# Layer 0's norms of pairs 2 to 4 applied to rows as they lie, in a bidirectional recurrence with a ternary feed-forward block

## The chip, the core and the metric

The kernel runs on one core of a Trainium2 chip. The core has five engines that work through their own instruction streams in order and wait for each other by semaphores: PE (TensorE, matrix products and transposes), DVE (VectorE), ACT (ScalarE), POOL (GpSimd) and SP (SyncE, which here only issues DMAs). The metric is the device time of one execution in microseconds. Before the change it was 1712.66 us, the median of 3 runs (1712.62 to 1712.66).

## The reference, cut to what matters

The input x is 8 sequences of 512 tokens with 512 channels. Three things are added up:

```python
x = x + xcond(layernorm(x))        # two stacks of 4 gated recurrent layers, one forward, one backward in time
x = x + ffn(layernorm(x))          # 512 -> 2048 -> 512, weights rounded to -1, 0, 1

def mingru(h, Wz, bz, Wh, bh):     # Wz = Wh and bz = bh here
    z = sigmoid(h @ Wz.T + bz);  a = clip(1 - z, 1e-8, 1 - 1e-8)
    return scan(a, z * tanh(h @ Wh.T + bh))      # s_t = a_t s_(t-1) + b_t along the tokens

def stack(h):
    for i in range(4):
        new = mingru(h, ...)
        if i > 0: new = new + h
        h = layernorm(new) * gamma + beta        # over the 512 channels of each token
    return h
```

All arithmetic is in float32. Both directions of a stack use the same weights, so in layer 0 they also share their products.

## The kernel before, in words

**Layout.** The recurrence keeps a sequence with channels on the 128 partitions and tokens along the row: 4 chunks of 128 channels by 512 tokens, since the scan of DVE runs along a row. A layernorm needs sums over channels, which lie across partitions. So a norm turns the 4 chunks round: for each of 4 tiles of 128 tokens, `turned` (L316) makes 4 transposes on PE into a PSUM tile `pt`, `stats` (L171 to L182) finds mean and variance on DVE and the power -1/2 on POOL, `normalise` (L188, L189) writes the token tile `tok` on ACT, and `back` (L325, L331) turns the 4 tiles into 4 channel chunks `pf` on PE and applies gamma and beta on ACT while it writes them to the state. A turn of one tile and a back of one chunk are 4 transposes of 128x128 each.

**Slots.** The order of the work is written out by the program, in slots (`slot`, `shares`, `queue`). A slot first emits its own work, mostly one chunk of a layer (`gates`, L487: 4 float32 products, recorded as 8 MATMULs, then two sigmoids and a tanh on ACT and the clip on POOL), then what is due in the list `stages`, then its shares: from the queue `turns` and from the queue `backs` each one piece if it is ready, and a second one if that is late (its time plus its piece number has come; `cap` is 2 in a slot of the fusion). After the shares come, on DVE, the product z*t (L514), the scan (L518) and the residual addition (L588) of the chunk. What DVE gets in a slot's shares is thus ahead of that slot's scan. A token tile that `last` writes in one slot can be turned back from the next slot on.

**Pairs.** The 8 sequences go in 4 pairs, and each pair has 4 streams (b, 0) and (b, 1), (b+1, 0) and (b+1, 1): sequence and direction. A layer takes 4 slots for each stream, so 16 for a pair. Between two pairs lies a transition: `fusion` of the old pair (8 tiles, L622, 16 MATMULs each, with two scaled additions L632 on DVE) is interleaved with `first_layer` of the new one (8 chunks, L535, with a scaling L546 and two scans). Numbered from the transition's start, slots 0 to 15 hold, in order, F C C F C F C C F C F C F C F F (F a tile of the fusion, C a chunk of layer 0). Slots 16 to 19 are layer 1 of the new pair's stream (b, 0), slots 20 to 23 of (b, 1), and so on. Layer 0's four norms run in slots 8 to 23: before the change (b, 0) and (b, 1) are turned in slots 8 to 12 and turned back in 11 to 15; (b+1, 0) and (b+1, 1) are turned in slots 15 to 19 and turned back in 18 to 23. Layer 1 of (b, 0) is next: its norm is queued for slot 21, is turned in slots 21 to 24, and its first chunk is turned back in slot 25.

**Buffers that tie the engines together.** `pt` has 2 PSUM tiles, `u` (the products) 4, the gate's tile `t` 2 and `a` 3, the tiles z 16, the token tiles `tok` 10.

**Other work in the order.** The rows of a sequence's own layernorm before layer 0 reduce to one factor for each token, `scale` (`scale_x`): 4 transposes of a broadcast column and one copy on ACT. For pairs 3 and 4 its statistics (`norm_x`) are found on DVE during layer 1 and 2 of the pair before, one tile in 4 slots from slot 21 on. The last norm of a stream (`norm_last`) needs only 1/sigma for each token; `by_scalar` finds it on ACT in two passes (L396 to L398), `tokens` on DVE. Rounding the feed-forward weights is cut into 68 steps (`extra`, done by `pieces(n)`): 32 sums, 4 for the two thresholds, 32 roundings. A rounding is two DVE instructions (L193, L194), with a load ahead and a store behind on SP's queue.

## Time and profile before

| what | value |
|---|---|
| median of 3 runs | 1712.66 us |
| profiled execution | 1712.95 us, its span 1711.2 us, clock granted to PE 1.00 |
| PE busy | 1700.3 us of the span (99%) |
| DVE busy | 1389.1 us (81%) |
| ACT busy | 1089.5 us (64%) |
| POOL busy | 377.2 us (22%) |
| transitions between pairs, slots 0 to 15 | about 262 to 357, 562 to 654, 860 to 952 us |
| feed-forward block | from 1218 us on |

The profile lists groups of instructions as line, engine, operation, `out<-in` by the program's tile names, shapes, count, busy time, mean duration in ns, and the idle time of the engine before them with what ended it. PE's instructions overlap in a pipeline: a MATMUL of 593 ns starts 430 ns after the one before, a transpose of 273 ns 109 ns after the one before, so a time on PE is best taken between starts. A row of the windows view gives a stretch, its length, and each engine's busy time with its count of instructions; a row of the timeline gives start, length, engine, line, operation, tiles and count.

### The profile page before, as it was taken

The numbers are of one execution on the slowest core, as the hardware profiler recorded it, in microseconds if no ns is written. First come the engines' busy times: TensorE is split into PE (matmuls) and PEld (weight loads), VectorE is DVE, ScalarE is ACT, GpSimd is POOL, SyncE is SP. The second block draws the span as 40 slices with busy tenths as digits, with TensorE's granted clock in tenths as the row PEclk, the third lists the DMA queues.
The fourth block names the chain that finished last, engine by engine and source line by source line (L and its number), as shares of the span: only waits on it lengthen the run. The fifth ranks groups of instructions, "written<-read, shape, count | busy, mean of one in ns | idle before, by whom it ended". The sixth has DMA issues, their size and how long they took to land.

```text
span 1711.2 us, 19776 instructions
## 1 busy us (share of the span) xinstructions
PE 1700.3 (99%) x6440; PEld 1042.6 (61%) x6440; DVE 1389.1 (81%) x2619; ACT 1089.5 (64%) x1918; POOL 377.2 (22%) x558
## 2 busy tenths in 40 slices
PE   9999999999999999999999999999999999999999
PEld 5455554555555455555545555554688888888887
DVE  7988889889887888888788888885568768768877
ACT  5898873468886346888535688862356566666654
POOL 3333333223332222333222222321000000000000
PEclk9999999999999999999999999999999999999999
DMA  7002231150000125000012200102201101100100
GB/s 271 19 25 81 98 93 37 66 193 19 13 1 1 56 68 191 19 13 1 1 56 75 98 28 22 75 1 99 74 1 50 50 1 50 50 21 30 50 19 31
DMA packets 46599, 91.75 MB, mean 54 GB/s; under 512 B 5280, under 2 KB 5536, under 8 KB 45472
## 3 DMA queue, kind: packets, MB, share of 16 engines
q1 hardware_dynamic: 45488, 88.78, 15.1%
q10 hardware_dynamic: 1008, 1.70, 0.3%
q8 instruction: 51, 0.84, 0.2%
q14 instruction: 52, 0.43, 0.1%
HBM read 65.30 MB, written 25.17 MB: 53 GB/s over the span
## 4 chain that ended last, share of the span: by engine, by line
PE 92%; DVE 5%; ACT 2%; POOL 1%; issue 0%; DVEq 0%
PE u L487 33%; PE po L937 14%; PE ph L910 14%; PE pu L622 13%; PE u L535 6%; PE pt L316 6%; PE pf L325 4%; DVE z L518 1%; PE py L214 1%; DVE z L514 1%; DVE st L171 1%; ACT tok L189 1%; DVE z L588 1%; PE pst L948 0%; POOL rs L178 0%
## 5 line engine op out<-in xcount | busy, mean ns | idle before, releaser
L487 PE MATMUL u<-xT,gw 128*128 128x512 f32 x768 | 345.5, 593 | 0.0
L487 PE MATMUL u<-h,gw 128*128 128x512 f32 x768 | 345.5, 592 | 0.0
L518 DVE TENSOR_TENSOR_SCAN z<-a,z 128x512 f32<-128x512 f32 x224 | 277.1, 1237 | 21.8 <-DVE z L514 0.9
L511 POOL TENSOR_SCALAR a<-a 128x512 f32<-128x512 f32 x224 | 150.3, 671 | 559.2 <-ACT a L505 558.3
L487 PEld LDWEIGHTS u<-xT,gw 128*128 128x128 f32 x768 | 138.6, 190 | 138.7 <-issue 137.0
L487 PEld LDWEIGHTS u<-h,gw 128*128 128x128 f32 x768 | 138.6, 190 | 138.2 <-issue 138.2
L505 ACT ACTIVATE a<-u,ngb 128x512 f32<-128x512 f32 x192 | 131.7, 686 | 142.4 <-PE u L487 140.9
L937 PE MATMUL po<-pwq,ghi 128*128 128x512 f32 x512 | 202.8, 396 | 0.0
L171 DVE BATCH_NORM_STATS2 st<-pt 128x6 f32<-128x512 f32 x244 | 169.3, 694 | 39.2 <-PE pt L316 32.5
L937 PE MATMUL po<-pwq,glo 128*128 128x512 f32 x512 | 199.7, 390 | 0.0
L910 PE MATMUL ph<-yhi,fcq 128*128 128x512 f32 x512 | 199.7, 390 | 0.0
L910 PE MATMUL ph<-ylo,fcq 128*128 128x512 f32 x512 | 199.4, 389 | 0.0
L514 DVE TENSOR_TENSOR z<-z,t 128x512 f32<-128x512 f32 x224 | 154.8, 691 | 52.6 <-ACT z L507 52.3
L914 ACT ACTIVATE g<-ph 128x512 f32<-128x512 f32 x128 | 76.4, 597 | 186.6 <-PE ph L910 186.6
L178 POOL TENSOR_TENSOR rs<-ve,mhalf 128x1 f32<-128x1 f32 x192 | 125.5, 654 | 155.1 <-DVE nmu L182 152.7
L189 ACT ACTIVATE tok<-pt,nmr,rs 128x512 f32<-128x512 f32 x192 | 149.4, 778 | 6.4
L925 DVE TENSOR_TENSOR acc<-acc,g 128x512 f32<-128x512 f32 x112 | 77.4, 691 | 85.0 <-ACT g L914 84.1
L507 ACT ACTIVATE z<-u,gb 128x512 f32<-128x512 f32 x192 | 132.4, 690 | 0.0
L506 ACT ACTIVATE t<-u,gb 128x512 f32<-128x512 f32 x192 | 130.8, 681 | 0.0
L316 PEld LDWEIGHTS pt<-ident,z 128*128 128x128 f32 x640 | 78.7, 141 | 77.2 <-issue 48.9
L535 PE MATMUL u<-xT,gw 128*128 128x512 f32 x256 | 114.8, 593 | 0.8 <-DVE gw L767 0.8
L622 PE MATMUL pu<-fw,xT 128*128 128x512 f32 x256 | 115.2, 593 | 0.0
(164 smaller groups left out, 2621.0 us busy)
## 6 DMA issues: line engine op xcount, KB each, us to landing
xf<-in_x_dram SPq DMA_DIRECT2D x32, 256.0 KB, 5.5
x<-xf SPq DMA_DIRECT2D x32, 256.0 KB, 2.0
xy<-x SPq DMA_DIRECT2D x32, 256.0 KB, 4.0
xn<-in_x_dram SPq DMA_DIRECT2D x31, 256.0 KB, 4.5
out_dram<-xy SPq DMA_DIRECT2D x31, 256.0 KB, 2.0
xT<-in_xt_dram SPq DMA_DIRECT2D x7, 1024.0 KB, 7.7
fca<-in_fc_wT_dram SPq DMA_DIRECT2D x16, 256.0 KB, 2.9
pwa<-in_proj_wT_dram SPq DMA_DIRECT2D x16, 256.0 KB, 2.6
```

The lines of the kernel that those rows point to most:

```text
L171: nc.vector.bn_stats(st, src)
L189: nc.scalar.activation(dst, src, AF.Identity, bias=nmr, scale=rs)
L316: nc.tensor.transpose(pt[:, ts(c, P)], zs[c][:, ts(t, P)], ident)
L487: nc.tensor.matmul(u, lhsT=gw[l][:, c, ts(o, P)], rhs=h[:, c, :], start=(c == 0), stop=(c == NC_ - 1),)
L507: nc.scalar.activation(z, u, AF.Sigmoid, bias=gb[:, l, o : o + 1])
L511: engine.tensor_scalar(a, a, CLAMP_HI, CLAMP_LO, ALU.min, ALU.max)
L514: nc.vector.tensor_tensor(z, z, t, ALU.mult)
L518: nc.vector.tensor_tensor_scan(dst[:, d], a[:, d], z[:, d], 0.0, ALU.mult, ALU.add)
L535: nc.tensor.matmul(u, lhsT=gw[0][:, c, ts(o, P)], rhs=xT[b][:, c, :], start=(c == 0), stop=(c == NC_ - 1),)
L622: nc.tensor.matmul(pu, lhsT=hs[d][:, c, ts(t, P)], rhs=fw[:, d * NC_ + c, :], start=(c == 0), stop=(c == NC_ - 1),)
L910: nc.tensor.matmul(ph, lhsT=w, rhs=ys[b][c][i], start=(c == 0 and i == 0), stop=(c == NC_ - 1 and i == 1),)
L937: nc.tensor.matmul(po[b][t], lhsT=part[:, ts(t, P)], rhs=pwq[k // NP_][:, k % NP_, :], start=(k == 0 and i == 0), stop=(k == NF - 1 and i ...
```

## The change

For layer 0's norms of sequences 2 to 7, except that of stream (b, 0) where b is even (so three norms in each of pairs 2, 3 and 4, nine in all), `norm_rows` takes the place of `norm`. The turns stay: each tile is still turned into `pt`. Tiles 0 and 1 get their mean and variance on ACT (two passes over the tile), tiles 2 and 3 on DVE, all into one small tile `pk` of 128 x 2 x 4. `close` makes 1/sigma of all four tiles at once (one addition on DVE, one power on POOL). One slot later `send` turns `pk` with a single transpose into 8 short rows, copies them on ACT, writes them to DRAM and reads them back twice as rows of 512 tokens broadcast to all 128 partitions (`to_rows`, three DMAs on SP's queue). Two slots after that (`LANDS`) the norm is applied to the chunks where they lie, with channels on partitions: for each chunk DVE subtracts the row of means and multiplies by the row of 1/sigma, in place, and one slot later ACT applies gamma and beta into the state. The token tiles, `normalise` and `back` go away for these nine norms. For the odd sequences the pieces are numbered two by two, so that up to two turns or two chunks are taken in a slot.

`scale_x` of sequences 2 to 7 goes through `to_rows` too. `norm_last` uses `by_scalar` for the streams (2, 0), (4, 0) and (6, 0) as well. Of the weight steps, a fusion now does 4 and not 12; the streams of sequences 2 to 5 do one in each layer, behind the slot of chunk 1.

```diff
--- before.py
+++ after.py
@@ -250,7 +250,14 @@
                 super().append(tile_)
                 self.at = now[0] + self.lag
 
+        class Rows:
+
+
+            at = None
+
         def ready(at):
+            if isinstance(at, Rows):
+                return at.at is not None and at.at <= now[0]
             if isinstance(at, Tokens):
                 return len(at) == NT and at.at <= now[0]
             return at <= now[0] and held[0] < TOK
@@ -265,7 +272,7 @@
                     if not q or not ready(q[0][0]):
                         break
                     at, piece = q[0][:2]
-                    late = (at.at if isinstance(at, Tokens) else at) + piece <= now[0]
+                    late = (at.at if isinstance(at, (Tokens, Rows)) else at) + piece <= now[0]
                     if i >= cap and not late:
                         break
                     some.append(take(q))
@@ -351,12 +358,94 @@
             for c in range(NC_):
                 queue(backs, s, toks, c // pair, back(toks, dst, c, True, f"{tag}_{c}"))
 
+        LANDS = 2
+
+        def to_rows(cols, n, dsts, tag):
+
+            turned_ = ps_f.tile([P, S], F32, tag="pf", name=f"prow_{tag}")[0 : n * NT, 0:P]
+            nc.tensor.transpose(turned_, cols.rearrange("p i t -> p (i t)"), ident)
+            short = dsts[0][0 : n * NT, 0:P]
+            nc.scalar.copy(short, turned_)
+            row = dram.tile([n, S], F32, tag=f"row_{tag}", name=f"row_{tag}")
+            nc.sync.dma_start(out=row.rearrange("i (t p) -> (i t) p", p=P), in_=short)
+            for i, dst in enumerate(dsts):
+                nc.sync.dma_start(out=dst, in_=row[i : i + 1, :].broadcast_to([P, S]))
+
+        def norm_rows(s, zs, tag, pause, pair=1):
+
+
+            rows_, at = Rows(), now[0] + pause
+            pk = small.tile([P, 2, NT], F32, tag="pk", bufs=6, name=f"pk_{tag}")
+            wide = []
+
+            def close():
+                nc.vector.tensor_scalar(pk[:, 1, :], pk[:, 1, :], LN_EPS, None, ALU.add)
+                nc.gpsimd.tensor_tensor(pk[:, 1, :], pk[:, 1, :], mhalf.broadcast_to([P, NT]), ALU.pow)
+                stages.append((now[0] + 1, "late", send))
+
+            def send():
+                for i in range(2):
+                    wide.append(tokp.tile([P, S], F32, tag="tok", name=f"wide{i}_{tag}"))
+                to_rows(pk, 2, wide, tag)
+                rows_.at = now[0] + LANDS
+
+            def turn(t):
+                source, name = turned(zs, t, f"{tag}_{t}"), f"{tag}_{t}"
+
+                def go():
+                    src = source()
+                    if t == 0:
+                        held[0] += 2
+                    if t >= 2:
+                        st = small.tile([P, 6], F32, tag="st", name=f"st_{name}")
+                        nc.vector.bn_stats(st, src)
+                        nc.vector.bn_aggr(pk[:, :, t], st)
+                        if t == NT - 1:
+                            close()
+                        return lambda: None
+
+                    def last():
+                        sm, ss = (small.tile([P, 1], F32, tag=k, name=f"{k}_{name}") for k in ("sm", "ss"))
+                        mean, var = pk[:, 0, t : t + 1], pk[:, 1, t : t + 1]
+                        nc.scalar.activation(src, src, AF.Copy, accum_out=sm)
+                        nc.scalar.activation(mean, sm, AF.Copy, scale=1.0 / H)
+                        nc.scalar.activation(src, src, AF.Square, bias=mean, scale=-1.0, accum_out=ss)
+                        nc.scalar.activation(var, ss, AF.Copy, scale=1.0 / H)
+                    return last
+                return go
+
+            def apply(c):
+
+                def go():
+                    nc.vector.tensor_tensor(zs[c], zs[c], wide[0], ALU.subtract)
+                    nc.vector.tensor_tensor(zs[c], zs[c], wide[1], ALU.mult)
+                    left[s] += 1
+                    if c == NC_ - 1:
+                        held[0] -= 2
+
+                    def last():
+                        left[s] -= 1
+                        zlive[0] -= 1
+                        if s not in state:
+                            state[s] = hp.tile([P, NC_, S], F32, tag="h", name=f"h_{s[0]}{s[1]}")
+                        nc.scalar.activation(
+                            state[s][:, c, :], zs[c], AF.Identity,
+                            bias=bet[:, c : c + 1], scale=gam[:, c : c + 1],
+                        )
+                    stages.append((now[0] + 1, "late", last))
+                return go
+
+            for t in range(NT):
+                queue(turns, s, at, t // pair, turn(t))
+            for c in range(NC_):
+                queue(backs, s, rows_, c // pair, apply(c))
+
         def norm_last(s, tag):
             rsv[s] = small.tile([P, NT], F32, tag="rsv", name=f"rsv_{tag}")
             zs = [state[s][:, c, :] for c in range(NC_)]
             for t in range(NT):
                 source, name = turned(zs, t, f"{tag}_{t}"), f"{tag}_{t}"
-                queue(turns, s, now[0] + NC_ + 1, t, by_scalar(s, t, source, name) if s[0] > 1 and s[0] % 2 and s[1] == 0 else
+                queue(turns, s, now[0] + NC_ + 1, t, by_scalar(s, t, source, name) if s[0] > 1 and s[1] == 0 else
                       tokens(source, None, rsv[s][:, t : t + 1], name))
 
         def by_scalar(s, t, source, name):
@@ -378,6 +467,13 @@
         rx, scale = {}, {}
 
         def scale_x(b):
+
+            def spread_x():
+                scale[b] = gp.tile([P, S], F32, tag="scale", bufs=2, name=f"scale_{b}")
+                to_rows(rx[b].unsqueeze(1), 1, [scale[b]], f"x{b}")
+
+            if b > 1:
+                return spread_x
 
             def go():
                 pf = ps_f.tile([P, S], F32, tag="pf", name=f"pr_{b}")
@@ -558,13 +654,13 @@
                             zf.append(f)
                             if o == NC_ - 1:
                                 state[b, 0] = xT.pop(b)
-                                norm((b, 0), zf, f"{b}0_0", 2 if b == 1 else 1, 2 if b < 2 else 1)
+                                (norm_rows if b > 1 and b % 2 else norm)((b, 0), zf, f"{b}0_0", 2 if b == 1 else 1, 2 if b < 2 or b % 2 else 1)
 
                             def backward():
                                 scan(z, a, z, True)
                                 zb.append(z)
                                 if o == NC_ - 1:
-                                    norm((b, 1), zb, f"{b}1_0", 2 if b == 1 else 1, 2 if b < 2 else 1)
+                                    (norm if b < 2 else norm_rows)((b, 1), zb, f"{b}1_0", 2 if b == 1 else 1, 2 if b < 2 or b % 2 else 1)
                             if b == 0:
                                 stages.append((now[0] + 1, "resid", backward))
                             else:
@@ -595,7 +691,7 @@
                             stages.append((now[0] + c, "resid", sums))
                 slot(gates(h, l, o, f"{s[0]}{s[1]}_{l}_{o}", scans))
 
-                if s[0] < 2 and (l == L - 1 or o % 2) and len(extra) > 2 * NW or s == (B - 1, 1) and l == L - 1:
+                if s[0] < 2 and (l == L - 1 or o % 2) and len(extra) > 2 * NW or 2 <= s[0] < 6 and o == 1 or s == (B - 1, 1) and l == L - 1:
                     pieces(1)
             now[0] -= 1
             if l < L - 1:
@@ -614,7 +710,7 @@
                         rs.extend(rsv.pop((b, d)) for d in range(2))
                     row = xs["f", b, t]
                     nc.vector.tensor_tensor(row, row, fb, ALU.add)
-                    pieces((1, 2, 1, 0, 1, 2, 2, 3)[t + (b % 2) * NT])
+                    pieces((0, 1, 0, 0, 0, 1, 1, 1)[t + (b % 2) * NT])
                     pus = []
                     for d in range(2):
                         pu = ps_u.tile([P, H], F32, tag="u", name=f"pu_{b}_{t}_{d}")
```

## The prediction

> **What bounds the kernel now.** First the page's busy times and its chain:
>
> ```profile
> PE 1700.3 (99%) x6440; PEld 1042.6 (61%) x6440; DVE 1389.1 (81%) x2619; ACT 1089.5 (64%) x1918; POOL 377.2 (22%) x558
> PE 92%; DVE 5%; ACT 2%; POOL 1%; issue 0%; DVEq 0%
> ```
>
> PE is busy 99% and carries 92% of the chain, so what leaves PE leaves the time, as long as no other engine makes PE wait. DVE is next. An average hides stages, so I asked for windows where the change puts its work: from the last fusion MATMUL of each of the three transitions (I call this moment zero) to the end of slot 26's products, and a whole first half, slots 0 to 15.
>
> ```profile
> core 0: us, PE busy (x) PEld busy (x) DVE busy (x) ACT busy (x) POOL busy (x), PEclk, DMA share, GB/s
> 356.59:405.03 48.44, 48.05 (x181) 26.23 (x180) 41.10 (x89) 38.29 (x66) 15.97 (x25) 1.00 0.37 128
> 654.33:702.80 48.47, 48.08 (x182) 26.25 (x181) 41.12 (x89) 38.29 (x66) 15.97 (x25) 1.00 0.37 127
> 952.07:1000.52 48.45, 48.06 (x181) 26.24 (x180) 40.05 (x83) 38.16 (x66) 14.73 (x23) 1.00 0.13 51
> ...
> 264.00:356.59 92.59, 92.59 (x288) 45.98 (x287) 80.15 (x144) 32.96 (x56) 19.42 (x27) 1.00 0.21 70
> ```
>
> The reader is to see that PE idles 0.39 us in each stretch of 48.4 us and not at all in the first half, and that DVE has 7.3 us free in the stretch (8.4 in the third). Then the timeline, for prices between starts:
>
> ```profile
> 375.74 3.60 PE L487 MATMUL u<-h,gw 128*128 128x512 f32 x8
> 379.18 0.60 PE L325 MATMUL pf<-ident,tok 128*128 128x128 f32 x4
> 379.62 3.60 PE L487 MATMUL u<-h,gw 128*128 128x512 f32 x8
> ...
> 355.05 0.49 DVE L193 TENSOR_SCALAR fcq<-fcb,lo_fc 128x512 f32<-128x512 f32 x1 [2.14 <-DMA wq_fc<-fcq]
> 355.57 0.75 DVE L194 SCALAR_TENSOR_TENSOR fcq<-fcb,hi_fc,fcq 128x512 f32<-128x512 f32 x1
> ...
> 381.26 0.69 DVE L514 TENSOR_TENSOR z<-z,t 128x512 f32<-128x512 f32 x1 [1.49 <-ACT z L507]
> 382.05 1.23 DVE L518 TENSOR_TENSOR_SCAN z<-a,z 128x512 f32<-128x512 f32 x1
> 383.31 0.69 DVE L588 TENSOR_TENSOR z<-z,h 128x512 f32<-128x512 f32 x1
> 383.92 0.69 DVE L171 BATCH_NORM_STATS2 st<-pt 128x6 f32<-128x512 f32 x1
> 384.65 0.18 DVE L173 BATCH_NORM_AGGREGATE mv<-st 128x2 f32<-128x6 f32 x1
> 384.86 0.16 DVE L177 TENSOR_SCALAR ve<-mv 128x1 f32<-128x1 f32 x1
> 384.93 0.15 DVE L182 TENSOR_SCALAR nmu<-mv 128x1 f32<-128x1 f32 x1
> 384.99 0.69 DVE L171 BATCH_NORM_STATS2 st_x<-xn 128x6 f32<-128x512 f32 x1
> ```
>
> A chunk's products take 3.44 us of PE, a turn or a back 0.44. On DVE a chunk's product, scan and addition take 383.92 - 381.26 = 2.66; a tile's statistics 384.99 - 383.92 = 1.07, of which statistics and aggregate alone 0.95; an x tile 1.0; a rounding 1.2.
>
> **What PE gains.** Nine norms lose 4 backs each: 36 x 0.44 = 15.7 us. Six `scale_x` lose 4 transposes each: 24 x 0.109 = 2.6 us. Fifteen single transposes come in; between the pitch of 0.109 us and the row's duration of 0.273 each, 1.6 to 4.1 us in all; nearest are pipelined transposes, I take 0.15 each, 2.2 us. Of the 36 backs, 27 lie in the three stretches above (9 each), the others in slots 13 and 14.
>
> **What DVE gets.** A norm's application is two operations on SBUF tiles for each chunk, a subtraction and a product, like L588. They depend on each other as product and scan do (0.79 between starts), and the next one follows after 0.61: 1.40 us a chunk, 5.6 a norm. (Were both 0.61 it would be 1.22; this is the low end.) Off go two tiles' statistics, 2.1 us, and the small operations of the others. Of the three applications in a transition, 2 of 12 chunks fall into slot 15, ahead of moment zero, where DVE has room; 10 fall into slots 16 to 22: two of stream (b, 1) in slots 16 and 17, then two in each of slots 19 to 22. All are ahead of the scans of their slots, and all ahead of the statistics of layer 1's first norm (slots 21 to 24), on which slot 25's first back waits. Two roundings (slots 17 and 21) come in as well in the first two transitions, and an x tile (slot 21) was there before.
>
> The walk along DVE, in us from moment zero. It is free at 1.6 (the fusion's last additions) and waits for slot 16's first turn, whose transposes end 4.3 + 0.44 + 0.2 = 4.9. Then, each slot's shares and its chunk:
> - 16: two tiles and `close` 2.05, a chunk 1.40, product to addition 2.66: to 11.1
> - 17: 1.40 + 2.66 + rounding 1.2: to 16.3
> - 18: 2.05 + 2.66: to 21.0
> - 19: 2.80 + 2.66: to 26.5
> - 20: 2.80 + 2.66: to 31.9
> - 21: 1.07 + 2.80 + x 1.0 + 2.66 + 1.2: to 40.7
> - 22: 1.07 + 2.80 + 2.66: to 47.2
> - 23: 1.07 + 2.66: to 51.0
> - 24: 1.07: to 52.1
>
> From there the power on POOL and `normalise` on ACT need 1.75 (as at 358.25 to 360.0), the back 0.44 and slot 26's chunk 3.44: the stretch ends at 57.7 and not 48.44, 9.3 later. PE alone would need 48.05 - 9 x 0.44 + 0.3 = 44.4. In the third transition there are no roundings and no x tile: 54.3, 5.9 later. **Sum of the stretches: 9.3 + 9.3 + 5.9 = 24.5 us lost**, the 27 backs already counted. PE reaches this by waiting: `t` lets ACT run two chunks ahead of DVE, then `pt`'s two tiles are not released, then the back waits for `tok`.
>
> **Outside the stretches:** 9 backs (3.9) and the scale rows (2.6) leave PE, 9 single transposes (1.35) come in: 5.2 us gained.
>
> **What I cost at nothing, and its cover.** Roundings leave the fusion: 8 x 1.2 = 9.6 us of DVE each time, but PE has no idle time there, so nothing comes back. In layers 1 to 3 of pairs 2 and 3 the roundings take DVE's room: 4 x 3.73 + 1.2 + 1.0 = 17.1 us against PE's 4 x 4.3 = 17.2. Their cover is that 0.1 and the slots between a norm's last tile and the rounding; if it is gone, at most 18 x 1.2 = 21.6 us. ACT's passes (L396 to L398, 1.63 us a tile from 569.36 to 570.99) for 12 tiles of `norm_last` lie in layer 3, where ACT has 20 us in 52 free. For 18 tiles of the new norms they hold `pt` in slot 17 until about 15.1 and PE waits 1.7 us in slot 18, inside the time that DVE takes anyway. The three DMAs of `send`: (b+1, 0)'s copy ends at 10.9 behind slot 17's activations, a 256 KB store lands in 2.0 and a load in 2.9 to 5.5, so rows stand at 16 to 18.5 and DVE comes at 21.0. On SP's queue they stand behind x loads that were issued at once, and behind them stand weight loads, x1 stores and later loads with slots to spare. The scale rows go out five slots, some 20 us, ahead of use.
>
> **A rule that speaks against the change.** DVE's tile operations with two SBUF inputs keep 0.688 to 0.693 us in these stretches although POOL is busy in a third of them. The Trainium skill, "SBUF — State Buffer", section "Who interferes with whom", has such a DVE instruction and a POOL one that reads SBUF exclude each other for their whole length. By the row the 20 new operations of a stretch cost nothing more; by the rule an estimate is 20 x 1/3 x 0.3 = 2 us a stretch, 6 in all.
>
> **Sum.** 1712.95 + 24.5 - 5.2 = 1732.2 for an execution like the profiled one; the median stands 0.3 below that: **1732 us**, slower by 1.1%. Low end of this case: chunks at 1.22, 10 x 3 x 0.18 = 5.4 less, and 2 for the small terms, 1724; high end: single transposes at 0.27, two waits more for each pair, 1739.
>
> **Rivals.**
> *The backlog never reaches PE (faster).* Place: slots 18 to 26. If DVE kept up, each stretch would take 44.4: 12.1 gained and 5.2 outside, 1695. For it: DVE idles 19% in the page, and in all of slots 0 to 26 it would still have room. Against: the windows show 41.1 of 48.4 taken, and 16.4 come in (ten chunks, two roundings) while 4.6 go (four tiles' statistics and the small operations). The sign turns where the 60 new operations in the stretches would take 19.3 us less, 0.32 each: at 0.38 us in place of 0.70.
> *The roundings find no room in the layers either (slower still).* Half of their bound, 11 us: 1743. For it: 17.1 against 17.2. Against: the same layers carry x tiles now with single waits of 0.4.
> *The rows land late.* If a read takes 8 us, as the first broadcast of `fb` did (8.7), (b+1, 0)'s rows stand at 21 to 22 and the walk shifts by up to 1.4 in each stretch: 1736.
>
> **How the numbers follow.** A measurement tells 0.2%, 3.4 us, from no change. The forecast has 0.68, late rows 0.06, the layers' rival 0.13: 0.87 slower. The fast rival has 0.11; halfway between, within 0.2%, 0.02. The range leaves out the fast rival and takes in the others: 1719 (a stall a third smaller than the walk gives) to 1746.
>
> **What would show it.** The stretch from the fusion's end to slot 26's products at 57 to 58 us twice and 54 once, with DVE over 93% busy in it and PE idle some 13 us, put down to `tok` on ACT or to DVE. `pf<-ident,tok` x624 and not x768, 72 subtractions and 72 products of 0.69 us on DVE, PE busy near 1683 in a longer span, slots 0 to 15 about 1.5 us shorter. Wrong would be: stretches at 45 us; idle PE in layers 1 and 2 behind roundings; or DVE's first idle time in slots 19 to 22 put down to a DMA.

## The result and the profile after

The changed kernel takes 1743.57 us (median of four runs, 1742.34 to 1744.80) against 1712.66 (1712.62 to 1712.87): 1.018 times as long, with a 95% interval of 1.0163 to 1.0198. That is 30.9 us lost where 19.3 were forecast; 1743.57 is inside the range. The profiled execution took 1743.5 with a span of 1741.7, 30.5 more than before's.

First the page's busy times and its chain:

```profile
PE 1699.6 (98%) x6287; PEld 1028.2 (59%) x6287; DVE 1408.7 (81%) x2568; ACT 1100.7 (63%) x2023; POOL 390.1 (22%) x531
PE 71%; DVE 20%; ACT 5%; issue 2%; POOL 1%; DMA 1%; DVEq 0%; ACTq 0%
```

PE's share of the chain fell from 92% to 71% and DVE's rose from 5% to 20%. The page's 81% for DVE is what it was before: an average over the whole span says nothing of what happened. The same windows as before, one for each stretch, and then the first half of the first transition (columns as in the prediction: length, busy time of each engine, granted clock, DMA share, GB/s):

```profile
355.07:413.15 58.08, 48.29 (x147) 23.40 (x146) 51.21 (x89) 39.56 (x79) 16.16 (x19) 0.94 0.26 82
664.67:724.44 59.77, 49.16 (x148) 23.47 (x146) 52.78 (x91) 39.90 (x79) 16.83 (x19) 0.94 0.24 80
974.48:1031.30 56.82, 49.02 (x148) 23.34 (x147) 49.08 (x81) 39.80 (x79) 15.38 (x17) 0.94 0.17 61
262.00:355.07 93.07, 92.77 (x282) 45.45 (x281) 73.13 (x124) 30.77 (x58) 18.48 (x25) 1.00 0.11 36
```

The stretches grew from 48.4 to 58.1, 59.8 and 56.8. PE now idles in them, and its granted clock, 1.00 before, is 0.94. PE's timeline of the first stretch shows where it waits (the lines with a wait, in brackets, and the chunk that follows the longest one):

```profile
370.21 0.66 PE L323 MATMUL pt<-ident,z 128*128 128x128 f32 x4 [1.23 <-ACT pt L412]
...
374.80 0.27 PE L366 MATMUL prow<-ident,pk 128*8 128x128 f32 x1 [0.51 <-POOL pk L383]
...
390.87 0.66 PE L323 MATMUL pt<-ident,z 128*128 128x128 f32 x4 [1.18 <-ACT tok L189]
...
399.65 1.12 PE L323 MATMUL pt<-ident,z 128*128 128x128 f32 x4 [4.69 <-ACT tok L189]
400.56 6.07 PE L583 MATMUL u<-xT,gw 128*128 128x512 f32 x8
...
409.55 0.33 PE L332 MATMUL pf<-ident,tok 128*128 128x128 f32 x1 [2.13 <-ACT tok L189]
409.72 3.60 PE L583 MATMUL u<-xT,gw 128*128 128x512 f32 x8
```

The waits are put down to ACT's `tok`, the next link behind DVE: ACT stood idle for 102.9 us in all before `nmr`, waiting for POOL's `rs` (27.9 before), and POOL's `rs` waits for DVE's `nmu`. On DVE itself the same moments read:

```profile
388.58 0.68 DVE L420 TENSOR_TENSOR z<-z,wide 128x512 f32<-128x512 f32 x1
389.29 0.69 DVE L421 TENSOR_TENSOR z<-z,wide 128x512 f32<-128x512 f32 x1
389.90 0.68 DVE L420 TENSOR_TENSOR z<-z,wide 128x512 f32<-128x512 f32 x1
390.62 0.69 DVE L421 TENSOR_TENSOR z<-z,wide 128x512 f32<-128x512 f32 x1
391.23 0.69 DVE L171 BATCH_NORM_STATS2 st_x<-xn 128x6 f32<-128x512 f32 x1
...
395.12 0.47 DVE L193 TENSOR_SCALAR fcq<-fcb,lo_fc 128x512 f32<-128x512 f32 x1
395.63 0.75 DVE L194 SCALAR_TENSOR_TENSOR fcq<-fcb,hi_fc,fcq 128x512 f32<-128x512 f32 x1
396.30 0.69 DVE L171 BATCH_NORM_STATS2 st<-pt 128x6 f32<-128x512 f32 x1
```

No line of it has a wait in brackets: DVE does two chunks' applications, an x tile, a chunk, a rounding, and only then the statistics that PE's turn at 399.65 waits for.

Where the 30.5 us went, by the times at which PE's chunks end in both traces:

| part | before | after | difference |
|---|---|---|---|
| start to the first stretch | 356.75 | 355.23 | -1.5 |
| stretch 1 | 48.45 | 58.08 | +9.6 |
| layers of pair 2 | 156.38 | 159.28 | +2.9 |
| slots 0 to 15, second transition | 92.92 | 92.23 | -0.7 |
| stretch 2 | 48.44 | 59.78 | +11.3 |
| layers of pair 3 | 156.38 | 157.81 | +1.4 |
| slots 0 to 15, third transition | 92.91 | 92.23 | -0.7 |
| stretch 3 | 48.45 | 56.82 | +8.4 |
| the rest | 710.48 | 710.26 | -0.2 |

The stretches lose 29.3, the layers 4.3, and 3.1 are gained elsewhere. In the layers the scale rows give back 0.65 for each pair (below), so that the roundings there cost 3.55 + 2.07 = 5.6.

### The profile page after: what moved, and what is told of

It reads as the page before. It is cut to its first block, busy times and chain, and to the rows that moved or that the text cites. A ratio compares the mean times of both kernels' runs of the same rounds, so it can differ in the third digit from the quotient of the medians.

```text
span 1741.7 us, 19581 instructions
## 1 busy us (share of the span) xinstructions
PE 1699.6 (98%) x6287; PEld 1028.2 (59%) x6287; DVE 1408.7 (81%) x2568; ACT 1100.7 (63%) x2023; POOL 390.1 (22%) x531
## 3 DMA queue, kind: packets, MB, share of 16 engines
q1 hardware_dynamic: 49136, 95.13, 16.3%
## 4 chain that ended last, share of the span: by engine, by line
PE 71%; DVE 20%; ACT 5%; issue 2%; POOL 1%; DMA 1%; DVEq 0%; ACTq 0%
PE u L583 18%; PE po L1033 13%; PE ph L1006 13%; PE pu L718 13%; PE u L631 6%; DVE z L614 6%; PE pt L323 4%; DVE z L610 3%; DVE st L171 2%; DVE z L684 2%; PE pf L332 2%; POOL rs L178 1%; ACT tok L189 1%; ACT z L603 1%; PE py L214 1%
## 5 line engine op out<-in xcount | busy, mean ns | idle before, releaser
L583 PE MATMUL u<-xT,gw 128*128 128x512 f32 x768 | 354.3, 605 | 0.0
L607 POOL TENSOR_SCALAR a<-a 128x512 f32<-128x512 f32 x224 | 162.4, 725 | 560.6 <-ACT a L601 559.5
L583 PEld LDWEIGHTS u<-xT,gw 128*128 128x128 f32 x768 | 142.5, 195 | 144.4 <-issue 142.7
L171 DVE BATCH_NORM_STATS2 st<-pt 128x6 f32<-128x512 f32 x196 | 135.7, 692 | 26.9 <-PE pt L323 23.7
L178 POOL TENSOR_TENSOR rs<-ve,mhalf 128x1 f32<-128x1 f32 x156 | 111.7, 716 | 138.4 <-DVE nmu L182 136.0
L188 ACT ACTIVATE nmr<-nmu,rs 128x1 f32<-128x1 f32 x156 | 47.0, 301 | 131.4 <-POOL rs L178 102.9
L189 ACT ACTIVATE tok<-pt,nmr,rs 128x512 f32<-128x512 f32 x156 | 121.3, 777 | 5.2
L323 PE MATMUL pt<-ident,z 128*128 128x128 f32 x640 | 97.2, 277 | 22.4 <-ACT tok L189 16.9
```

The source lines that it names most:

```text
L171: nc.vector.bn_stats(st, src)
L189: nc.scalar.activation(dst, src, AF.Identity, bias=nmr, scale=rs)
L323: nc.tensor.transpose(pt[:, ts(c, P)], zs[c][:, ts(t, P)], ident)
L583: nc.tensor.matmul(u, lhsT=gw[l][:, c, ts(o, P)], rhs=h[:, c, :], start=(c == 0), stop=(c == NC_ - 1),)
L607: engine.tensor_scalar(a, a, CLAMP_HI, CLAMP_LO, ALU.min, ALU.max)
```

## The experiments

Line numbers of the short diffs are left out. The runs are numbered 1 to 12 in the order in which they were planned. Stretches are given as their three lengths, of before 48.4 each. Runs 1 to 4 and 6 to 8 are one execution each; the changed kernel's four times span 2.5 us, so a smaller difference than that is read from the stretches of the traces and not from the whole time.

**1. What do the roundings cost in the layers?** Two runs: the changed kernel with the weight steps of before, and the kernel before with the weight steps of the change.

```diff
 # first run, from the kernel after
-                    pieces((0, 1, 0, 0, 0, 1, 1, 1)[t + (b % 2) * NT])
+                    pieces((1, 2, 1, 0, 1, 2, 2, 3)[t + (b % 2) * NT])
 ...
- or 2 <= s[0] < 6 and o == 1
 # second run, from the kernel before: the same two lines the other way round
```

> The changed kernel with the weight steps put back as before (12 in a fusion, none behind the layers' second slots); norms on rows, scale rows and by_scalar stay. Theory 1 (roundings cost time in the layers because DVE's room there is too small, whether or not a backlog came before): the 3.5 us lost in the layers of pair 2 and the 2.1 us in those of pair 3 go, and the first two stretches (fusion's end to slot 26's products) lose 2.4 us of DVE work each; 1731 to 1736 us. Theory 2 (the layers' losses are an echo of the transitions' backlog): the steps of 0.5 us for each stream stay, only the stretches get shorter; 1738 to 1740 us.

> The kernel before with nothing changed but the weight steps spread over the layers. Theory 1: PE waits about 0.5 us for each stream in layers 1 and 2 of pairs 2 and 3, the transitions stay at 48.4 us; 1716 to 1719 us. Theory 2: DVE has room without the backlog; 1712 to 1713 us.

Alone, the spread roundings cost 7.5 us: 1720.14 against 1712.61. Six of these arise in the layers of pairs 2 and 3 (156.38 becomes 159.37 and 159.36), where PE waits at a back once in every round of four slots, which takes 17.73 us instead of 17.23. This has nothing to do with a backlog from a transition: there is none in this kernel. DVE's timeline in one such layer:

```profile
424.39 0.69 DVE L588 TENSOR_TENSOR z<-z,h 128x512 f32<-128x512 f32 x1
425.00 0.83 DVE L193 TENSOR_SCALAR fcq<-fcb,lo_fc 128x512 f32<-128x512 f32 x1
425.87 0.75 DVE L194 SCALAR_TENSOR_TENSOR fcq<-fcb,hi_fc,fcq 128x512 f32<-128x512 f32 x1
426.54 0.69 DVE L171 BATCH_NORM_STATS2 st<-pt 128x6 f32<-128x512 f32 x1
```

and POOL's at the same place:

```profile
424.54 1.01 POOL L511 TENSOR_SCALAR a<-a 128x512 f32<-128x512 f32 x1 [1.11 <-ACT a L505]
```

The rounding takes 426.54 - 425.00 = 1.54 us and not 1.2, since its first instruction takes 0.83 and not 0.48. It has 0.83 to 0.92 in the layers' slots where it begins with POOL's clamp or while it is running, seven times in a row in each of the two pairs, and 0.48 where the clamp begins later or no clamp runs (371.11, clamp from 371.43). With 1.54, and one wait of 0.18 for ACT's `z`, DVE's round of four slots with an x tile is 17.7 us (420.26 to 438.00, from statistics to statistics), longer than PE's 17.23, and PE follows DVE. Without the wait and the extra 0.35 it would be 17.2, which is no cover either. No run moved the rounding to a place without the clamp.

In the changed kernel, taking the roundings out of the layers brought only 2.3 us (1741.24, above both ranges that were expected). The layers did get their 5.6 back (155.73 each), but the stretches became 59.36, 60.51 and 58.13. DVE's timeline of that run around moment zero (354.9) shows why:

```profile
351.94 0.49 DVE L193 TENSOR_SCALAR fcq<-fcb,lo_fc 128x512 f32<-128x512 f32 x1 [1.89 <-DMA wq_fc<-fcq]
...
355.52 0.49 DVE L193 TENSOR_SCALAR fcq<-fcb,lo_fc 128x512 f32<-128x512 f32 x1 [1.02 <-DMA wq_fc<-fcq]
356.05 0.75 DVE L194 SCALAR_TENSOR_TENSOR fcq<-fcb,hi_fc,fcq 128x512 f32<-128x512 f32 x1
356.71 0.69 DVE L420 TENSOR_TENSOR z<-z,wide 128x512 f32<-128x512 f32 x1
```

Three roundings in the last fusion slot, two of them waiting for the store of an earlier one, now stand ahead of two chunks' applications, and the backlog begins before moment zero. So a rounding costs time in either place once DVE is full: spreading them was no free move, and leaving them was none either.

**2. Is it DVE's work in the stretch, or the rows' arrival, or ACT's passes?** The subtraction was left out (so this kernel's norms lack their means, and its time is that of less work), or given to POOL; and all four tiles' statistics were given to DVE, which takes ACT's passes away and adds 1.9 us of DVE to a norm.

```diff
 # third run: left out; seventh run: nc.gpsimd in its place, and the weight steps of before
-                    nc.vector.tensor_tensor(zs[c], zs[c], wide[0], ALU.subtract)
 # eighth run
-                    if t >= 2:
+                    if t >= 0:
```

> The changed kernel without the subtraction of the row of means (the computation leaves the mean out of nine norms): of the 20 new DVE operations in each stretch 10 go, 7.1 us. Theory A (DVE's backlog sets the stretches): they end at about 51, 51 and 47.5 us, PE's clock stays at 1.00 since no wait is longer than 3 us, and the layers still lose 5 to 6 us; 1716 to 1721 us. Theory B (DVE is not it: the rows land late, or ACT's two passes hold the PSUM tiles): less than 5 us come back; over 1738 us.

> The changed kernel with the statistics of all four tiles of a norm on DVE, none by ACT's two passes. Theory A (DVE's backlog sets the stretches): 4 tiles of 0.95 us more in each stretch, 3.8 us; stretches of 61 to 64 us twice and 58 to 61 once; 1752 to 1757 us. Theory B (PE waits for the PSUM tiles that ACT's passes hold, 1.2 us in each stretch): faster than 1743.

> The changed kernel with the weight steps back in the fusion and the subtraction of the means moved from DVE to POOL (nothing left out). Theory A: DVE loses 7.1 us in each stretch as without the subtraction, and 2.4 more in the first two by the roundings: stretches of 48 to 51 us, 1710 to 1720 us in all, if POOL keeps up: it has 32 us free in a stretch, so 10 subtractions may take up to 3 us each. If POOL's subtractions hold up its clips or DVE's operations on two SBUF tiles, the stretches stay over 54 us: over 1728.

Without the subtraction: 1725.09, stretches 53.40, 51.69 and 50.61, where about 51, 51 and 47.5 were expected. The clock did not stay at 1.00 either: in the first and the third stretch it was halved for 3.4 us behind a wait of 2.13 us, and the chunk there ended 1.7 us later than in the second. Without these 1.7 the stretches would be 51.7, 51.7 and 48.9. Run 4 below, the changed kernel with the clock held at 1.00, has 58.11, 58.10 and 55.14: the 30 subtractions are worth 19.0 us, 0.63 each, nearly the 0.71 to 0.73 that most of them take from their start to the product's. So a stretch is as long as DVE's work in it. The time is 4 us above its range by the two slow pieces and a third stretch 1.4 longer than expected; the layers, which this edit does not touch, lose 1.5 and 3.2 in it, where 5 to 6 were expected. With two more statistics of each norm on DVE: 1753.74, inside its range, stretches 62.9, 63.8 and 60.8. If ACT's passes had held PE up, this run would have been the faster one.

On POOL the subtraction made it worse still: 1768.92, stretches 67.6, 69.1 and 68.9, where 1710 to 1720 was the hope and run 1, the same kernel with the subtraction on DVE, took 1741.24. POOL takes 1.26 to 1.76 us for one, DVE then waits for it, and there is a second cost. POOL's and DVE's timelines of this run:

```profile
384.16 3.27 POOL L420 TENSOR_TENSOR zf<-zf,wide 128x512 f32<-128x512 f32 x2
```

```profile
381.87 2.75 DVE L421 TENSOR_TENSOR zf<-zf,wide 128x512 f32<-128x512 f32 x2 [3.83 <-POOL zf L420]
384.55 1.76 DVE L610 TENSOR_TENSOR z<-z,t 128x512 f32<-128x512 f32 x1
386.34 2.17 DVE L614 TENSOR_TENSOR_SCAN z<-a,z 128x512 f32<-128x512 f32 x1
```

While POOL works on its two subtractions (384.16 to 387.43), DVE's product takes 1.76 and not 0.69, its scan 2.17 and not 1.23. So work moved from DVE to POOL was partly still paid on DVE.

**3. What does the clock cost?** In the changed kernel PE's waits fall together with a lower granted clock. Windows around the waits of the three stretches:

```profile
391.30:410.00 18.70, 11.88 (x32) 5.71 (x30) 17.61 (x33) 11.24 (x21) 6.07 (x7) 0.82 0.27 84
700.00:726.00 26.00, 17.89 (x50) 8.74 (x51) 24.54 (x47) 16.46 (x29) 9.02 (x11) 0.87 0.19 61
1009.00:1033.00 24.00, 18.13 (x51) 8.53 (x51) 21.63 (x41) 16.65 (x29) 7.34 (x9) 0.86 0.00 0
```

0.18 x 18.7, 0.13 x 26 and 0.14 x 24 are each 3.4 us lost, that is 6.7 us at half the clock. An experiment fills PE's waits with products whose results nothing reads (1, 5, 1 and 2 of them at four places in slots 23 to 25, fewer in the third transition), so that PE's queue stays busy while DVE's work is unchanged.

```diff
+                pf = ps_f.tile([P, S], F32, tag="pf", name=f"fill_{kind}_{name}")
+                for _ in range(n):
+                    nc.tensor.matmul(pf, lhsT=ones, rhs=fw[:, 0, :], start=True, stop=True)
```

> The changed kernel with idle products put on PE where it waits in slots 23 to 25 (9 in each of the first two transitions, 6 in the third, 0.86 us each; the results are read by nobody). If the halved clock of PE after its long waits costs time of its own (theory C), the clock stays at 1.00, the second and the third stretch get about 2 us shorter each and the first at most 0.5; 1738.5 to 1740.5 us. If the halved clock lies inside DVE's time anyway (theory D), 1743 to 1744 us. If the filling is in PE's way, slower than 1744.5.

The clock stayed at 1.0 throughout, and the stretches are 58.11, 58.10 and 55.14. Against the changed kernel that is nothing in the first, 1.7 less in each of the others: there the last chunk of the stretch ran slow (719.31: 5.30 us and not 3.60), and behind it no wait is left that could take it up. In the first the slow chunk (400.56: 6.07) stands ahead of a wait. The whole time, 1742.17, lies between the two ranges, because the layers of pair 3 lost 1.5 more than in the changed kernel. What a backlog of DVE costs the stretches without the clock is therefore 9.7 + 9.7 + 6.7 = 26.0 us, and the clock 3.3. In the whole time holding the clock brought only 1.4 us, less than the changed kernel's times lie apart: while PE runs slowly DVE catches up, and the layers of pair 3 gain back 1.5 of it.

**4. The scale rows alone**, in the kernel before, with `by_scalar`:

```diff
-                                (norm_rows if b > 1 and b % 2 else norm)((b, 0), zf, ...)
+                                norm((b, 0), zf, ...)
 # the same for (b, 1), and the weight steps of before
```

> The kernel before with the scale rows and by_scalar alone, no norm on rows, weight steps as before. The prediction's step: 24 transposes of 0.109 us leave PE, 6 of 0.15 come in, by_scalar costs nothing: 1.7 us less, 1710.5 to 1711.2. If by_scalar makes PE wait for its tiles in layer 3, or the scale rows come late: 1712.6 or more.

PE's last product ends 2.35 us earlier (1.1 of it before the first stretch, 0.65 in the layers of pair 2 and as much in those of pair 3), but the execution is as long as before: 1712.92, which the second case of the expectation has, but not for that case's reason. Behind the last stores this trace lists an instruction transfer (`q8 instruction`) that before's last 9 us do not have. It is one execution of one kernel; the runs below that have the scale rows too lack this tail, and what brought it is left open. From PE's last product to the end it is 6.1 us here and 3.6 to 3.8 in every other run.

**5. Is there a number of row norms that DVE can hide?** The remaining runs put one norm of each transition on the rows, that of (b, 1) with b even, whose chunks can be applied in slots 14 to 16.

```diff
-                                (norm_rows if b > 1 and b % 2 else norm)((b, 0), zf, ...)
+                                norm((b, 0), zf, ...)
-                                (norm if b < 2 else norm_rows)((b, 1), zb, ...)
+                                (norm if b < 2 or b % 2 else norm_rows)((b, 1), zb, ...)
-        LANDS = 2
+        LANDS = 1
 # weight steps of a fusion, by run; "or 2 <= s[0] < 6 and o == 1" is gone in all
+ run 5        (2, 2, 2, 2, 1, 1, 1, 1)
+ run 9        (1, 2, 1, 0, 1, 2, 2, 3)                                  as before
+ runs 10, 11  (1, 2, 1, 0, 2, 3, 2, 1) if b < 2 else (2, 2, 1, 0, 2, 2, 2, 1)
+ run 12       (1, 2, 1, 0, 2, 3, 3, 0) if b < 2 else (2, 2, 1, 0, 2, 3, 2, 0)
 # runs 10 to 12: all four statistics on DVE (t >= 0); runs 11 and 12: the four chunks in one slot
-                queue(backs, s, rows_, c // pair, apply(c))
+                queue(backs, s, rows_, 0, both(c))   # c = 0, 2; both(c) applies c and c + 1
```

> A version that should beat both: of the three norms of a transition only that of stream (b, 1) goes to the rows, its application is moved one slot ahead (rows used one slot after they are sent), so that all of it falls into slots 14 and 15, ahead of the fusion's end, where DVE has room; the weight steps are back in the fusion, two in each of its first four tiles and one in each of the last four; scale rows and by_scalar stay. Theory A (DVE's backlog in slots 16 to 24 is the loss, the transposes taken from PE are a gain wherever DVE keeps up): 4 backs of 0.44 us for each of 3 transitions and 2.0 for the scale rows come back, less 0.5 for single transposes: 5.5 to 7 us less than before, 1705.5 to 1707.5. Rival (a norm on rows costs PE in itself, by its rows' way through DRAM or by ACT's passes): 1712 or more.

> One norm of each transition on the rows (that of (b+1, 0)'s partner which lies earliest, `(b, 1)` with b even), its passes one slot after the rows are sent, the scale rows, and the weight steps of the fusion exactly as before the change. Theory: the 17 us that the earlier version of this lost were its weight steps (two roundings just ahead of the first new turns: PE waited 1.93 us there, and the threshold's product was pulled to a place where PE waited 6.25 us), and not the norm. Then the fusions fall by 0 to 0.7 us each, the stretches rise by 1.1 to 3.5 each, because up to three roundings now stand ahead of slot 16, and the scale rows give 1.7: 1711 to 1719. Rival: the norm on the rows costs this by itself, through ACT's passes that hold `pt`: 1725 or more.

> As the run beside it, but all four tiles' statistics of the norm on DVE instead of two on ACT, and the twelve weight steps of a transition dealt out with at most one in the last fusion slot and none ahead of the first new turns. DVE then carries 2.1 us more for a norm ahead of slot 16, and 1.2 to 2.4 less just ahead of it. If room on DVE in slots 13 to 15 is all that the idea needs, four backs (1.76 us) leave PE in each transition and each stretch costs at most 1.1 more: 1707 to 1713, not slower than before. If the application's 5.6 us of DVE can't be hidden even for one norm: 1714 to 1720.

> One norm on the rows with all its statistics on DVE, as before, but its four chunks are applied in one slot behind the rows' arrival, so that nothing of the application is left for slot 16. In the run before this two chunks (2.7 us of DVE) stood in slot 16 behind two tiles' statistics, and PE waited 1.5 to 2.2 us for `pt` in slot 18; the stretches rose by 1.1 to 2.2. If that wait comes from those 2.7 us, DVE is now up to 1.9 us late at slot 16's statistics instead, and on time after them: each stretch rises by 0 to 1.2 and the time is 1708 to 1712. If DVE's total up to slot 18 decides and not its order, the wait stays: 1711.5 to 1713.5.

> As the run beside it, and the last fusion slot's rounding (1.2 us of DVE) is dealt out to slots 11 to 14, where DVE has room. DVE is then at most 0.7 us late at slot 16's statistics and early behind them: the wait in slot 18 goes, each stretch at -0.5 to 0.5, and with the fusions' 1.2 and the layers' 0.65 the time is 1706 to 1710, faster than before by 0.15 to 0.4%. If the earlier roundings make PE wait in slots 11 to 14 instead, as they did once: 1711 or more.

| run | time, us | ratio and interval | slots 0 to 15, second transition | stretches |
|---|---|---|---|---|
| before | 1712.66 | | 92.9 | 48.4, 48.4, 48.4 |
| 5 | 1729.50 | 1.0099 (1.0081 to 1.0117) | 94.6 | 49.6, 49.6, 49.6 |
| 9 | 1726.56 | 1.008 (1.0064 to 1.0097) | 92.2 | 53.8, 54.4, 54.1 |
| 10 | 1712.37 | 0.9999 (0.999 to 1.0008) | 91.7 | 49.6, 50.7, 49.8 |
| 11 | 1714.37 | 1.001 (1.0001 to 1.0019) | 91.7 | 49.9, 51.3, 50.7 |
| 12 | 1719.12 | 1.0036 (1.0024 to 1.0049) | 92.1 | 57.4, 50.1, 48.9 |

Run 5 missed its expectation (1705.5 to 1707.5) by its own weight steps. PE waits 6.25 us for the weights' threshold, which they had moved, in the first transition, and 1.93 us behind two roundings just ahead of the first turns; the part up to the first stretch grows by 11.1.

Run 9 put the weight steps back, and lost nearly as much. Its 1726.56 is in the range of the rival, but not by the rival's mechanism: PE waits 0.30 us for ACT's passes in a transition, no more. What is late is DVE again:

```profile
354.79 0.75 DVE L194 SCALAR_TENSOR_TENSOR fcq<-fcb,hi_fc,fcq 128x512 f32<-128x512 f32 x1
355.46 0.48 DVE L193 TENSOR_SCALAR fcq<-fcb,lo_fc 128x512 f32<-128x512 f32 x1
355.98 0.75 DVE L194 SCALAR_TENSOR_TENSOR fcq<-fcb,hi_fc,fcq 128x512 f32<-128x512 f32 x1
358.69 0.49 DVE L193 TENSOR_SCALAR fcq<-fcb,lo_fc 128x512 f32<-128x512 f32 x1 [1.96 <-DMA wq_fc<-fcq]
359.21 0.75 DVE L194 SCALAR_TENSOR_TENSOR fcq<-fcb,hi_fc,fcq 128x512 f32<-128x512 f32 x1
359.88 0.69 DVE L171 BATCH_NORM_STATS2 st<-pt 128x6 f32<-128x512 f32 x1
```

Three roundings and a wait of 1.96 us for a store stand ahead of slot 16's statistics, which begin at 359.88; in run 10, with one rounding there, they begin at 356.04. PE waits 3.27, 3.88 and 3.66 us in slot 17, and its clock is halved for 3.4 us in each of these places.

Run 10 is the best: as fast as before (the interval spans 1). PE is busy 1694.6 us, 5.7 less than before, the slots up to 15 gain 1.2 in each transition, the scale rows 0.65 in each pair's layers, and the stretches give 1.1 to 2.2 back, in one wait of 1.46 to 2.15 us in slot 18. Run 11 asked whether that wait comes from the order, two chunks' applications behind moment zero, and did all four ahead of it: the wait moved to slot 17 (1.00 and 1.72 us) and the time rose to 1714.37, above both of its ranges. That fits the case that DVE's sum up to slot 18 counts and not its order, but a second cause stands beside it: late rows. With `LANDS = 1` DVE stands idle for `wide` in slot 14, while in the changed kernel no application waits for its rows. In run 11 these waits, 0.83, 2.38 and 1.76 us, differ from transition to transition as the stretches do, and so do run 12's in the second and third (2.28 and 1.03). In run 11's second transition DVE works without a wait from the rows' landing (648.48) to the statistics that PE's turn in slot 17 waits for. Part of what one norm costs here is thus its rows' arrival; no run took this wait away. Run 12 took the last rounding away from there and lost 8.9 us in the first stretch to something else (its line numbers are 4 higher than the changed kernel's):

```profile
344.22 0.75 DVE L194 SCALAR_TENSOR_TENSOR fcq<-fcb,hi_fc,fcq 128x512 f32<-128x512 f32 x1
351.94 0.49 DVE L193 TENSOR_SCALAR fcq<-fcb,lo_fc 128x512 f32<-128x512 f32 x1 [6.97 <-DMA wq_fc<-fcq]
```

DVE stands 6.97 us, because its third rounding needs the buffer of an earlier one, whose store is in SP's queue. The issues of that queue at this moment:

```profile
344.01 0.28 SPq L370 DMA_DIRECT2D row<-wide  x1
345.26 0.81 SPq L372 DMA_DIRECT2D wide<-row  x2
346.12 0.42 SPq L746 DMA_DIRECT2D fcb<-in_fc_wT_dram  x1
346.64 0.38 SPq L779 DMA_DIRECT2D wq_fc<-fcq  x1
```

The pool has two buffers (L79), so the third rounding of slot 14 needs that of the first, which DVE left at 343.8. Its store is issued at 346.64: SP had waited 2.5 us for ACT's copy of the short rows and 0.9 us for `row` to land, and only then came to it; the third rounding's own load, issued at 346.12, had stood in the same queue. Another 5.3 us pass until DVE goes on, beside loads of rows and weights. So the rows' DMAs hold up what is behind them on SP. In the second and third transition slot 14 has two roundings and not three, none waits for a store, and the stretches are 50.1 and 48.9: there one norm is nearly hidden. Run 12's 1719.12 is in the range of its second case (1711 or more), but not by PE's waits in slots 11 to 14. Two roundings in the first as well were not tried. A version that beats the kernel before was not found; what one norm on the rows could bring is bounded by the 5.7 us that run 10 takes off PE's busy time.

## Why the prediction was right, and where it was off

**The mechanism and the walk: right.** "The stretches 57 to 58 us twice and 54 once, put down to `tok`": with the clock held, 58.1, 58.1 and 55.1. The walk's stations against DVE's timeline of the first stretch, from moment zero at 355.07: slot 16 ends at 11.1 (forecast 11.1), 17 at 16.2 (16.3), 18 at 21.2 (21.0), 19 at 26.7 (26.5), 20 at 32.4 (31.9), 21 at 41.2 (40.7), 22 at 47.8 (47.2), 24 at 52.7 (52.1), the stretch at 58.08 (57.7). No line of DVE in slots 19 to 22 waits for a DMA, so the late rows were no rival here; the cover held.

Inside that walk two errors partly cancelled. A chunk's application took 1.33 between starts and not 1.40 (376.25 to 377.57, for instance), some 0.8 less in a stretch. And six operations of each stretch were stretched by POOL, as at 375.24 (addition 1.09 and not 0.69), 383.11 (a subtraction, 1.10) and 400.81 (scan 1.45 and not 1.23): 1.7, 1.7 and 1.5 us more, 4.8 in all. Here the prediction had a rule of the Trainium skill ("SBUF — State Buffer", section "Who interferes with whom": DVE with two SBUF inputs and POOL reading SBUF exclude each other) against its row, took the row, 0 us, and noted 6 us by the rule. In size the rule was nearer, though not where it was applied: the 6 us were for the new operations, and only 4 of the 18 lengthened ones are new (1.4 us). The row misled because in before's stretches not one such operation is longer than usual, though POOL is as busy: there the slots' order keeps the two engines' operations apart, and the change moved DVE against POOL. Outside the stretches the trace of before has 15 of DVE's operations that begin inside a clamp, and all 15 are longer.

**The sum of the stretches: 24.5 forecast, 26.0 without the clock, 29.3 measured.** 1.5 is the walk's (the third stretch, 54.3 forecast against 55.1, makes 0.8 of it), 3.3 the halved clock, which no step of the prediction has. It was not to be seen in a trace whose clock is 1.00 all through; what was to be seen was that PE would wait.

**"Roundings in the layers cost nothing": the step that failed.** Its cover was said to be 0.1 us, "17.1 against 17.2", with 21.6 us as the bound if it were gone. It was gone: 5.6 us in the changed kernel, 7.5 alone. The term that was mis-sized is the rounding in that place, 1.54 us and not 1.2, because POOL's clamp runs beside it there. The trace of before had such a row: one rounding, at 319.21, took 0.83 for its first half. The rival "the roundings find no room in the layers either", priced at half the bound, 11 us, was the true one at half its price, and added to the forecast would have given 1738 to 1740. With it one of the prediction's own signs of being wrong came true: PE idle in layers 1 and 2 behind roundings.

**Outside the stretches: 5.2 forecast, 4.4 measured**, with the layers' 1.3 from the scale rows counted here (1.52 + 0.69 + 0.69 + 1.30 + 0.2). Single transposes and a wait of 0.3 us in slot 11 (328.02, for ACT's passes) take most of the rest. With 26.0 - 24.5, 3.3, 5.6 and 0.8 the miss of 11.2 us in the profiled execution is accounted for.

**Inside the range, with luck.** The forecast's own case ended at 1739; 1743.57 is above that, and lies in the range only because the range took in the rivals up to 1746. It meets the layers' rival's 1743 by chance: the roundings are half of what was missing, and the clock, the walk and the small terms the other half.

**The signs.** `pf` x624 came. The stretches' DVE share was 88, 88 and 86% and not over 93, PE's idle time in them 9.8, 10.6 and 7.8 us and not some 13, slots 0 to 15 were 0.7 us shorter and not 1.5. PE was busy 1699.6 us and not near 1683; 8.8 of that are products at half the clock (`u<-xT` 354.3 us, 345.5 before), and the rest was not broken down. "72 subtractions and 72 products" counts each operation twice: nine norms of four chunks have 36 of each, as the trace shows.

**The fast rival: wrong, and by its own condition.** It needed operations of 0.38 us; they took 0.69, and with half of them left out (the subtractions) the kernel was still 12.5 us slower than before. Sending one norm and not three came out even.

## What to carry to other kernels

When work is moved off the engine that bounds a kernel, the price is set by the stretch where the work arrives: walk the receiving engine through that stretch in the order of its queue, and see when the first thing is late that the bounding engine needs; the page's average (DVE 81% before and after) shows nothing of it. A cover of 0.1 us in 17 is no cover: price the moved piece at the duration it has beside its new neighbours, another engine's operation in the same slot among them. And put a transfer that must wait for a chain of engines behind the stores that others are waiting for, since its queue works in order; no run here tried that order.

## What the runs showed of the hardware

- **POOL and DVE slow each other.** DVE's product of two SBUF tiles took 0.69 alone and 1.76 while POOL subtracted two tiles, the scan 1.23 and 2.17; a rounding's first half, a comparison of one SBUF tile with scalars, took 0.48 alone and 0.83 to 0.92 beside POOL's clamp. The Trainium skill's page "SBUF — State Buffer", section "Who interferes with whom", describes both, the second for DVE's two-port modes; these rows agree with it, though no trace here shows in which mode the comparison runs. The price is regular. In the changed kernel's trace 43 of these operations (on the tiles z and the weights) begin inside a clamp, and all 43 are longer, by what is left of the clamp less some 0.15 us: 0.37 left make 0.22 more, 0.55 left make 0.35 to 0.41. A clamp that begins inside one of them is longer in the same way (0.38 us left: 0.85 and not 0.61), and one that begins inside a statistics, which reads a single tile, keeps its 0.61.
- **The clock halves after shorter waits than expected, and not after every longer one.** The third stretch, where no wait was longer than 2.51 us:

```profile
1016.11 0.77 PE L323 MATMUL pt<-ident,z 128*128 128x128 f32 x4 [2.51 <-ACT tok L189]
1016.67 5.22 PE L583 MATMUL u<-xT,gw 128*128 128x512 f32 x8
...
1025.99 0.33 PE L332 MATMUL pf<-ident,tok 128*128 128x128 f32 x1 [2.13 <-ACT tok L189]
1026.16 5.29 PE L583 MATMUL u<-xT,gw 128*128 128x512 f32 x8
```

The two chunks took 5.22 and 5.29 us instead of 3.60. The Trainium skill's page "TensorE: Matmul & The Clock Gate", section "Why this matters for your kernels", puts the limit at gaps of about 3 us; here a single wait of 2.51 or 2.13 us, with only transposes next to it, was enough, and in run 5 one of 1.93 (326.60). But the wait of 2.13 us at 409.55 in the first stretch was followed by a chunk of 3.60, and in run 7 waits of 3.21 us (706.20 and 1023.35) by a full clock. So the length of one wait does not decide it. Filling the waits with idle products kept the clock at 1.0.
- **A queue works in order, and a store behind waiting DMAs starts late**: 2.8 us late in run 12 (343.8 to 346.64), of the 8.1 until its buffer was free.
